# Sync waits between the indirect DMAs of GpSimd, in a kernel of two graph layers

## The chip, the cores and the metric

The kernel runs on one core of one Trainium2 chip. The metric is device time in microseconds (us) of one execution; a kernel is timed in several runs and the median is compared. Engines are named as the profile names them: PE (TensorE matmul), PEld (its weight load), DVE (VectorE), ACT (ScalarE), POOL (GpSimd), SP (SyncE).

## The reference

Sixteen graphs of 1024 nodes with 64 channels go through two residual layers. Each layer begins with a layer norm and a ReLU.

```python
# --- layer 0 ---
h = jnp.maximum(_layernorm(x, axis=-1), 0.0)
x = x + _L0_gnn_ref(h, adj, nodemask, W1, b1, W2, b2)
# --- layer 1 ---
h = jnp.maximum(_layernorm(x, axis=-1), 0.0)
x = x + _L1_gnn_ref(h, adj, ...)
```

Layer 0 thins out the edges of every node with over ten neighbours, and then takes, for each node and each channel, three quantiles (0.25, 0.5, 0.75) over the node's remaining neighbours; their weighted sum is the aggregate:

```python
vals = jnp.where(nd[..., None], x[:, None, :, :], jnp.inf)
s = jnp.sort(vals, axis=2)
for tau, w in zip(TAUS, WTS):
    ...
    agg = agg + w * (v_lo + frac * (v_hi - v_lo))
out = (1.0 + EPS_GIN) * x + agg
y = jax.nn.relu(out @ W1 + b1) @ W2 + b2
```

Layer 1 is three graph convolutions over the full adjacency, relu(adj @ (x @ W) + b) with a batch norm after each, and a last matmul over the three results.

## The kernel before

The graphs are worked in eight pairs. `prepare` loads the adjacency of a pair, thins the edges, counts each node's remaining neighbours and sorts the nodes by that count, so that nodes with few neighbours stand first. `place` holds the sorted place of each node. Nodes are then sorted in groups with a fixed number of slots, one slot for one neighbour's row.

Most groups (`BLOCKS`, `TAIL`) are gathered by one-hot matmuls on PE (`gather`, L1180, from selections made on DVE at L1149). Three groups of nodes (`NODES`, with 17, 19 and 21 slots) are gathered by indirect DMA instead. `fetch_nodes` makes the tile `g_nodes` and a generator `ask`: for each slot k and each of the G parts a of the group (G = 2) it issues one indirect DMA from POOL (L1293) that fetches 128 rows of 64 floats from `rows_d` in DRAM by the indices in `rows_listed`. There are 20 such series over the kernel (`NODE_ORDER`), 744 DMAs in all. `weave` interleaves the steps of these generators with the steps of the sorting networks on DVE (L1087), by shares of the work that are written down in the calls. `sorted_by[0]` is the newest DVE instruction of a sorting network at the time a step is asked for; the first DMA of a slot (a == 0) is made to wait for it, except in the first series, which is asked for before any sorting has begun. `sort_nodes` sorts the rows of `g_nodes`.

The aggregates go to DRAM (`agg_d`) in sorted order. For layer 1, `later` runs beside the last sorting: its function `load` fetches the aggregates of a pair back into node order with one indirect DMA for each of the eight row tiles t of each of the two graphs x, 16 per pair and 128 in all (L1486), within `tc.high_priority()`. `first_layer` adds them to h (L1383), and `next_layer` does the convolutions (L1441).

Other work is issued from POOL too: `live_d` (L894, an indirect scatter of the thinned adjacency into sorted order) and `lp` (L909, its reload).

The instructions are written in the order of the program text, and a scheduler then sets the order on each engine from the dependences and priorities. A dependence can be added by hand with `tc.add_manual_dep`; of the class Sync it becomes a wait on a semaphore. DMAs of POOL use eight completion semaphores in turn.

Of the kernel before, what the change touches and what calls it, by code (L numbers as in the profile page):

```python
# [407 lines left out]
def graph_layers_kernel(ctx: ExitStack, tc: tile.TileContext, ins, out: bass.AP):  # L408
    nc = tc.nc
# [183 lines left out]
    def rows_of(ap):  # L593
        return ap.rearrange("(t p) c -> p t c", p=P)
# [426 lines left out]
    def view(bufs, spec, n1, n2, inner=None):  # L1021
# [20 lines left out]
            dims += [[s2 * W, n2]] * (n1 == 1 and n2 == 1) + [[inner, W // inner], [1, inner]]  # L1042
        return bass.AP(tensor=ap.tensor, offset=ap.offset, ap=dims)

    plans = {}
    sorted_by = [None]

# [232 lines left out]
    def fetch_nodes(pairs, i, pools, tag):  # L1280

        work, ps, rows = pools
        j0, j1, _, slots = NODES[i]
        G = len(pairs) if i == 2 else 2
        pool = work if tag == "s" else keep if tag == "r0" else rows
        g = pool.tile([P, slots, G * C], F32, tag=tag, bufs=2 if tag == "s" else 1, name="g_nodes")

        def ask():
            for k in range(slots):
                for a in range(G):  # L1290
                    st = pairs[a if i == 2 else 0]
                    at = 4 if i == 2 else 2 * a + i
                    asked = nc.gpsimd.indirect_dma_start(  # L1293
                        out=g[:, k, a * C : (a + 1) * C],
                        out_offset=None,
                        in_=rows_d[st.p][:, :],
                        in_offset=bass.IndirectOffsetOnAxis(ap=st.listed[:, at, k : k + 1], axis=0),
                    )
                    if a == 0 and sorted_by[0] is not None:
                        tc.add_manual_dep(  # L1300
                            asked.ins, sorted_by[0].ins.name,
                            mybir.DependencyInfo(mybir.DependencyClass.Sync, mybir.DependencyReason.DATA),
                            reason="rows are asked for one by one",
                        )
                yield

        z = work.tile([P, len(TAUS), G], F32, tag="z_nodes", bufs=2, name="z_nodes")
        for a in range(G):
            st = pairs[a if i == 2 else 0]
            at = 4 if i == 2 else 2 * a + i  # L1310
            nc.scalar.copy(z[:, :, a : a + 1], st.nodes_z[:, :, at : at + 1])
        return pairs, i, g, z, Steps(ask())

    def asking(fetched, first, end, share=1.0):
# [63 lines left out]
    def first_layer(pools, xt, h, agg, mask):  # L1378


        one, ps = pools
        X = xt.shape[2]
        nc.vector.tensor_tensor(agg, agg, h, ALU.add)  # L1383
        oT = channels_first(pools, agg, "chan")
        yield
        for x in range(X):
            rows = slice(x * C, (x + 1) * C)
            hT = one.tile([HID, N], F32, tag="hT", name="hT")
            for hf in range(NH):
                sl = slice(hf * HALF, (hf + 1) * HALF)  # L1390
                pm = ps.tile([HID, HALF], F32, tag="mm", name="pm1")
                nc.tensor.matmul(out=pm, lhsT=w1[rows, :], rhs=oT[rows, sl], start=True, stop=True)
                nc.scalar.activation(hT[:, sl], pm, AF.Relu, bias=b1)
            py = ps.tile([P, NT, C], F32, tag="mm", name="py")
            for t in range(NT):
                nc.tensor.matmul(out=py[:, t, :], lhsT=hT[:, t * P : (t + 1) * P], rhs=w2, start=True, stop=True)
            nc.vector.tensor_tensor(h[:, :, x, :], py, b2[:, None, :].to_broadcast([P, NT, C]), ALU.add)
            yield
        nc.vector.tensor_tensor(h, h, mask[:, :, :, None].to_broadcast([P, NT, X, C]), ALU.mult)
        nc.vector.tensor_tensor(xt, xt, h, ALU.add)  # L1400
        flat = "p t x c -> p (t x) c"
        layernorm_relu(one, agg.rearrange(flat), xt.rearrange(flat), h.rearrange(flat), NT * X)
        yield
        return channels_first(pools, agg, "chan")
# [64 lines left out]
    def later(pools, keep, done):  # L1469

        one, ps = pools


        def load(p):
            assert p < done.sent
            xt = one.tile([P, NT, 2, C], F32, tag="xt", bufs=2, name="xt")
            h = one.tile([P, NT, 2, C], F32, tag="h", name="h_late")
            agg = one.tile([P, NT, 2, C], F32, tag="agg", name="agg")
            mk = one.tile([P, NT, 2], U8, tag="mk", name="mk")
            for x in range(2):  # L1480
                b = 2 * p + x
                nc.sync.dma_start(out=xt[:, :, x, :], in_=rows_of(x_d[b]))
                nc.sync.dma_start(out=h[:, :, x, :], in_=rows_of(h_d[b][:, :]))
                with tc.high_priority():
                    for t in range(NT):
                        nc.gpsimd.indirect_dma_start(  # L1486
                            out=agg[:, t, x, :],
                            out_offset=None,
                            in_=agg_d[b][:, :],
                            in_offset=bass.IndirectOffsetOnAxis(ap=place[:, b, t : t + 1], axis=0),  # L1490
                        )
                nc.sync.dma_start(out=mk[:, :, x], in_=mask_d[b])
            return xt, h, agg, mk

        def first(xt, h, agg, mk):
            mask = one.tile([P, NT, 2], F32, tag="mask", name="mask")
            nc.vector.tensor_copy(mask, mk)
            cur = yield from first_layer(pools, xt, h, agg, mask)
            return xt, cur

        def second(p, x2, cur):
            adjT = []
            for x in range(2):
                adjT.append(one.tile([P, NT, N], F8, tag=f"adjT{x}", name=f"adjT{x}"))
                nc.sync.dma_start(out=adjT[x], in_=adjT_d[2 * p + x][:, :, :])
            yield
            yield from next_layer(pools, [out[2 * p], out[2 * p + 1]], adjT, x2, cur)

        loaded = load(0)
        yield  # L1510
        given = yield from first(*loaded)
        for p in range(NP):
            now = Steps(second(p, *given))
            now.step()
            yield
            ahead = None
            if p + 1 < NP:
                loaded = load(p + 1)
                for _ in range(5):
                    now.step()  # L1520
                    yield
                ahead = Steps(first(*loaded))
            while now.step():
                yield
                if ahead is not None and ahead.step():
                    yield
            if ahead is not None:
                ahead.rest()
                given = ahead.result
# [146 lines left out]
    with ExitStack() as stack:  # L1676
# [56 lines left out]
        with ExitStack() as inner:  # L1733
            one = inner.enter_context(tc.tile_pool(name="late", bufs=1))
# [89 lines left out]
```

## Time and profile before

| | us |
|---|---|
| median of 3 runs | 2872.86 |
| lowest, highest | 2872.21, 2877.92 |
| the profiled execution, time | 2872.55 |
| the profiled execution, span from first to last instruction | 2870.7 |
| DVE busy | 2347.0 (82% of the span) |
| PE busy | 2095.5 (73%) |
| ACT busy | 1584.5 (55%) |
| POOL busy | 1517.0 (53%) |

The busy rows of POOL are almost wholly [...] its DMAs: 1123.2 us for `g_nodes`, 189.4 us for `live_d`, 139.0 us for `agg`. The bytes themselves move on the 16 DMA engines, whose mean load is low (the queue of POOL's DMAs takes 9.0% of the 16 engines' span). A row such as "[0.30 <-issue]" behind an instruction tells how long its engine was idle before it, and what ended that.

### The profile page before, as it was taken

Reading aid. Unit: us, or ns where it says so; the run is one execution under the profiler, and the core shown is the slowest. Engines: PE = TensorE matmul, PEld = TensorE weight load, DVE = VectorE, ACT = ScalarE, POOL = GpSimd, SP = SyncE. Lnnn points to the kernel's source line nnn. Section 1 sums busy time; section 2 is a strip of 40 time slices with the busy share of each in tenths; the row PEclk is TensorE's granted clock in tenths of the full one; section 3 lists DMA queues with packets and bytes.
Section 4 is the critical chain, followed back from the end, with each engine's and each line's share of the span. In section 5 each row is a group of like instructions: output and inputs, shape, how many; then the busy total and the mean of one; then the engine's idle time right before and its main releaser. Section 6 shows DMA issues by size and latency. Waiting matters only on the chain.

```text
span 2870.7 us, 59053 instructions
## 1 busy us (share of the span) xinstructions
PE 2095.5 (73%) x23402; PEld 1450.2 (51%) x23402; DVE 2347.0 (82%) x5475; ACT 1584.5 (55%) x3316; POOL 1517.0 (53%) x1155
## 2 busy tenths in 40 slices
PE   1576986996888688778744985898488396437868
PEld 0344763674565366447522663675366263224545
DVE  3217999999989999999999999999699396637943
ACT  2775776687468568847762687588333133122222
POOL 5115374475838546572834275655855748862220
PEclk9888997998999799889966997999798798768989
DMA  3313222332322242233230322322310341211221
GB/s 98 107 33 103 82 77 58 110 89 65 95 74 73 59 116 86 57 79 99 77 77 12 104 89 74 111 74 64 79 26 14 76 82 52 41 39 45 61 60 46
DMA packets 261055, 205.57 MB, mean 72 GB/s; under 512 B 217121, under 2 KB 217249, under 8 KB 256673
## 3 DMA queue, kind: packets, MB, share of 16 engines
q1 hardware_dynamic: 165120, 131.39, 15.8%
q0 software_dynamic: 39680, 62.23, 9.0%
q10 hardware_dynamic: 55968, 8.09, 1.7%
q8 instruction: 185, 3.03, 0.4%
q14 instruction: 102, 0.83, 0.1%
HBM read 148.82 MB, written 52.75 MB: 70 GB/s over the span
## 4 chain that ended last, share of the span: by engine, by line
DVE 31%; PE 13%; POOL 8%; DMA 8%; ACT 7%; issue 4%; ACTq 0%; POOLq 0%; DVEq 0%; SPq 0%
DVE s L1149 5%; DVE t L1087 4%; POOL g_nodes L1293 4%; PE pg L1441 4%; POOL agg L1486 4%; DVE t_nodes L1087 3%; PE pg L1180 3%; DVE g L1087 2%; DVE g_pairs L1087 2%; DVE t_pairs L1087 2%; DMA a<-in_adj 2%; DVE g_nodes L1087 2%; ACT stays L883 2%; DMA g_nodes<-rows_d,rows_listed 2%; DMA agg<-agg_d,place 2%
## 5 line engine op out<-in xcount | busy, mean ns | idle before, releaser
L1293 POOL DMA_INDIRECT g_nodes<-rows_d,rows_listed x744 | 1123.2, 1510 | 874.4 <-DVE prod L1099 312.5
L1180 PE MATMUL pg<-s,hp 128*64 128x248 bf16 (+6 forms) x12048 | 883.0, 299 | 206.2 <-DVE s L1149 151.1
L1180 PEld LDWEIGHTS <-hp 128*64 128x64 bf16 x12048 | 645.6, 113 | 383.0 <-ACT hp L696 76.4
L1149 DVE TENSOR_SCALAR s<-r 128x3200 bf16<-128x3200 bf16 (+19 forms) x856 | 407.4, 525 | 25.9 <-PE pg L1180 23.7
L1441 PE MATMUL pg<-adjT,xw 128*64 128x512 fp8e4 x2304 | 279.1, 391 | 39.9 <-ACT xw L1430 32.7
L894 POOL DMA_INDIRECT live_d<-edge,place x128 | 189.4, 1480 | 146.9 <-DVE place L886 109.1
L1486 POOL DMA_INDIRECT agg<-agg_d,place x128 | 139.0, 1086 | 190.7 <-DMA agg_d<-agg_nodes 59.1
L1441 PEld LDWEIGHTS <-xw 128*64 128x64 bf16 x2304 | 135.7, 112 | 165.3 <-ACT xw L1430 39.6
L1185 ACT COPY g<-pg 128x248 f32<-128x248 f32 (+3 forms) x238 | 97.0, 408 | 213.1 <-PE pg L1180 212.3
L781 ACT ACTIVATE edge<-a 128x1024 fp8e4<-128x1024 uint32 x128 | 135.5, 1058 | 92.3 <-DMA a<-in_adj 75.5
L788 PE MATMUL ptE<-ident_h,one 128*128 128x128 bf16 x1024 | 84.8, 233 | 114.9 <-DVE one L785 69.2
L1087 DVE TENSOR_TENSOR t<-g 128x800 f32<-128x800 f32 (+9 forms) x184 | 167.5, 923 | 0.8
L1087 DVE TENSOR_TENSOR g<-t 128x992 f32<-128x992 f32 (+7 forms) x176 | 160.2, 931 | 2.0
L864 ACT ACTIVATE edge<-q,bias 128x1024 fp8e4<-128x1024 f32 x128 | 142.2, 1112 | 31.4 <-PE q L859 31.1
L1383 DVE TENSOR_TENSOR agg<-agg,h_late 128x1024 f32<-128x1024 f32 x8 | 9.8, 1229 | 182.2 <-DMA agg<-agg_d,place 182.2
L883 ACT ACTIVATE stays<-keys,minus 128x1024 fp8e4<-128x1024 f32 x128 | 143.1, 1118 | 27.2 <-PE keys L875 26.1
L837 ACT ACTIVATE stays<-cs,back 128x1024 f16<-128x1024 f32 x128 | 137.5, 1113 | 28.3 <-PE cs L833 17.0
L791 ACT ACTIVATE edgeT<-ptE 128x1024 fp8e4<-128x1024 f32 x128 | 131.2, 1028 | 15.5 <-PE ptE L788 14.6
L788 PEld LDWEIGHTS <-one 128*128 128x128 fp8e4 x1024 | 66.0, 104 | 140.2 <-DVE one L785 86.3
L1087 DVE TENSOR_TENSOR t_nodes<-g_nodes 128x256 f32<-128x256 f32 (+6 forms) x192 | 124.2, 658 | 14.4 <-DMA g_nodes<-rows_d,rows_listed 13.8
L929 PE MATMUL pt<-ident_h,lp 128*128 128x128 bf16 x1024 | 88.2, 239 | 58.9 <-ACT liveT L932 30.2
L1445 ACT ACTIVATE xT<-pg,c_L_gnn_b 128x512 f32<-128x512 f32 x48 | 32.9, 686 | 176.6 <-PE pg L1441 176.6
(245 smaller groups left out, 4622.2 us busy)
## 6 DMA issues: line engine op xcount, KB each, us to landing
a<-in_adj SPq DMA_DIRECT2D x128, 512.0 KB
adjT_d<-edgeT SPq DMA_DIRECT2D x16, 1024.0 KB
lp<-live_d POOLq DMA_DIRECT2D x32, 512.0 KB
adjT<-adjT_d SPq DMA_DIRECT2D x16, 1024.0 KB
g_nodes<-rows_d,rows_listed POOLq DMA_INDIRECT x744
room<-in_x SPq DMA_DIRECT2D x16, 256.0 KB
h_d<-room SPq DMA_DIRECT2D x16, 256.0 KB
rows_d<-room SPq DMA_DIRECT2D x64, 64.0 KB
```

Of the source, the lines that this page charges most:

```text
L781: nc.scalar.activation(edge[:, t, :], a[:, :].bitcast(U32), AF.Sign, accum_out=found[:, 0, b, t : t + 1], saturate=False)
L788: nc.tensor.matmul(out=pt[:, u, :], lhsT=one[:, u * P : (u + 1) * P], rhs=ident_h, start=True, stop=True)
L837: nc.scalar.activation(stays[:, t, :], cs, AF.Abs, bias=back[:, t : t + 1], scale=2.0)
L864: nc.scalar.activation(edge[:, t, :], q, AF.Relu, bias=bias(-2.0), accum_out=nv[:, t : t + 1], saturate=False)
L883: nc.scalar.activation(junk, keys, AF.Sign, bias=minus[:, t : t + 1], accum_out=above[:, t : t + 1], saturate=False)
L894: sent = nc.gpsimd.indirect_dma_start(out=live_d[b][:, :], out_offset=bass.IndirectOffsetOnAxis(ap=place[:, b, t : t + 1], axis=0), in_=ed ...
L1087: sorted_by[0] = nc.vector.tensor_tensor(view(bufs, o, n1, n2), view(bufs, a, n1, n2), view(bufs, b, n1, n2), ALU.max if op else ALU.min)
L1149: nc.vector.tensor_scalar(s[:, k, :, us, w0:], r[:, :, us, at + w0 : at + W], float(LIVE + 1 + k0 + k), None, ALU.is_equal)
L1180: summed = nc.tensor.matmul(out=pg[x * C : (x + 1) * C, ks, w0:], lhsT=st.hp[:, part, x, u, :], rhs=s[:, ks, x, u, w0:], start=(whole and ...
L1293: asked = nc.gpsimd.indirect_dma_start(out=g[:, k, a * C : (a + 1) * C], out_offset=None, in_=rows_d[st.p][:, :], in_offset=bass.IndirectO ...
L1441: nc.tensor.matmul(out=pg[cs, :], lhsT=part[:, u, cs], rhs=adjT[x][:, u, sl], start=(u == 0 and k == 0), stop=(u == NT - 1 and k == len(xw ...
L1486: nc.gpsimd.indirect_dma_start(out=agg[:, t, x, :], out_offset=None, in_=agg_d[b][:, :], in_offset=bass.IndirectOffsetOnAxis(ap=place[:, b ...
```

## The change

A helper `wait_for` makes one instruction wait for another with a Sync dependence. The wait for `sorted_by[0]` now goes through it. In `ask`, the first DMA of every odd slot from slot 3 on is also made dependent on `last`, the DMA issued just before it in the program text. In `load`, the DMA of row tile t = 4 of each graph is made dependent on that of row tile t = 3. In the changed file the lines of `ask` stand 8 lower (L1301) and that of `load` 7 lower (L1493).

```diff
+    def wait_for(one, other):
+
+        tc.add_manual_dep(
+            one.ins, other.ins.name,
+            mybir.DependencyInfo(mybir.DependencyClass.Sync, mybir.DependencyReason.DATA),
+            reason="indirect DMAs come with pauses",
+        )
+
...
                     if a == 0 and sorted_by[0] is not None:
-                        tc.add_manual_dep(
-                            asked.ins, sorted_by[0].ins.name,
-                            mybir.DependencyInfo(mybir.DependencyClass.Sync, mybir.DependencyReason.DATA),
-                            reason="rows are asked for one by one",
-                        )
+                        wait_for(asked, sorted_by[0])
+                    if a == 0 and k % 2 and k > 1:
+                        wait_for(asked, last)
+                    last = asked
                 yield
...
                 with tc.high_priority():
                     for t in range(NT):
-                        nc.gpsimd.indirect_dma_start(
+                        asked = nc.gpsimd.indirect_dma_start(
                             out=agg[:, t, x, :],
                             out_offset=None,
                             in_=agg_d[b][:, :],
                             in_offset=bass.IndirectOffsetOnAxis(ap=place[:, b, t : t + 1], axis=0),
                         )
+                        if t == 4:
+                            wait_for(asked, last)
+                        last = asked
                 nc.sync.dma_start(out=mk[:, :, x], in_=mask_d[b])
```

## The prediction, as it was made before the changed kernel had run

> **What bounds the kernel now.** I read four views in this order: the page's chain that ended last (where an added wait could count at all), the costliest groups (what POOL's indirect DMAs cost), the waits (who waits for their landing), and the time line of POOL with the piecewise chain around the DMAs that the change touches.
>
> ```profile
> PE 2095.5 (73%) x23402; PEld 1450.2 (51%) x23402; DVE 2347.0 (82%) x5475; ACT 1584.5 (55%) x3316; POOL 1517.0 (53%) x1155
> DVE 31%; PE 13%; POOL 8%; DMA 8%; ACT 7%; issue 4%; ACTq 0%; POOLq 0%; DVEq 0%; SPq 0%
> L1293 POOL DMA_INDIRECT g_nodes<-rows_d,rows_listed x744 | 1123.2, 1510 | 874.4 <-DVE prod L1099 312.5
> L1486 POOL DMA_INDIRECT agg<-agg_d,place x128 | 139.0, 1086 | 190.7 <-DMA agg_d<-agg_nodes 59.1
> ```
>
> DVE is the busiest engine and holds the largest share of the chain. POOL is busy half the time and holds 8% of the chain: in places it does set the pace. The last two rows (count, busy us, mean ns, idle before) give what one indirect DMA costs POOL, 1510 ns for a row of `g_nodes` and 1086 ns for one of `agg`.
>
> Now the waits (total us, times, longest) of POOL and of DVE:
>
> ```profile
> POOL g_nodes L1293 <- DMA g_nodes<-rows_d,rows_listed: 22.3, 73, 0.3
> POOL agg L1486 <- DMA agg<-agg_d,place: 5.5, 18, 0.3
> DVE agg L1383 <- DMA agg<-agg_d,place: 182.2, 8, 64.1
> ```
>
> POOL's indirect DMAs already wait for earlier ones: with eight completion semaphores in turn, each waits for the one eight issues ahead. The longest such idle is 0.3 us, the ordinary gap between two issues, so that wait never held POOL. The third row is where POOL's pace does count: DVE stands still 182.2 us in all, once for each pair, until the last of that pair's 16 `agg` DMAs has landed.
>
> **The change, step by step.** What counts is how the built program places the waits, so I read the changed kernel's instruction order with its waits against the old one. On PE, ACT, DVE and SP the instructions stand in the same order. On POOL there are 22 more semaphore-wait instructions (590 for 568) and a local reordering. Three things differ from what the diff suggests.
>
> First, only one of the 20 `g_nodes` series is changed, the first, whose DMAs do not wait for `sorted_by`. In the other 19 the built program keeps only the wait for DVE, on the same instructions and values as before; the second dependence leaves no wait. So there are 7 new waits (slots 3, 5, ... 15 of 17) and 16 for `agg` (two for each of 8 pairs), 23 and not 172: series of 17, 19 and 21 slots would hold 7, 8 and 9 waits, and 8 x 7 + 8 x 8 + 4 x 9 + 16 = 172.
>
> Second, in all 23 the scheduler has moved four other indirect DMAs between the one waited for and the one that waits. The waiting one is issued fifth behind it, not next.
>
> Third, the order of the `agg` DMAs within a pair is permuted, but the waits for the aggregates' stores still stand on the first of the 16, and the DVE add needs all 16.
>
> *Price of one wait.* The pace of issue and the time to landing, from the last `agg` group (time line of POOL, then the chain in order of time: start, us, what):
>
> ```profile
> 2769.24 0.94 POOL L1486 DMA_INDIRECT agg<-agg_d,place  x1 [0.30 <-issue]
> 2770.48 0.94 POOL L1486 DMA_INDIRECT agg<-agg_d,place  x1 [0.30 <-issue]
> 2771.73 0.94 POOL L1486 DMA_INDIRECT agg<-agg_d,place  x1 [0.31 <-issue]
> ...
> 2771.73 2.52 DMA agg<-agg_d,place
> ...
> 2039.16 4.96 DMA g_nodes<-rows_d,rows_listed
> ```
>
> One issue every 1.25 us (0.94 busy, 0.30 gap); landing 2.52 us after the issue began. A wait for the DMA just ahead would cost 2.52 - 1.25 = 1.27 us. A wait for the fifth ahead asks for something that was issued 5 x 1.25 = 6.25 us ago and landed 3.7 us ago: it costs nothing. The slowest landing on the chain, 4.96 us while other loads ran, still leaves 1.3 us; and where an issue between them is slower than 0.94 us, the distance grows with it. Cost of 23 waits: 0. What hides them is those four issues; without them it would be 16 x 1.27 = 20 us on DVE's wait for `agg`.
>
> *Price of an extra semaphore instruction.* In the second series the ninth DMA waits for one semaphore and the tenth for two, so that a separate semaphore instruction stands before the tenth:
>
> ```profile
> 342.08 1.66 POOL L1293 DMA_INDIRECT g_nodes<-rows_d,rows_listed  x1 [0.30 <-issue]
> 344.04 1.67 POOL L1293 DMA_INDIRECT g_nodes<-rows_d,rows_listed  x1 [0.30 <-DVE g L1087]
> L1486 POOLq EVENT_SEMAPHORE  x29: 17/43/25597, 2042.3 to 2753.2; - x29
> ```
>
> Both gaps are 0.30 us, so the instruction hides in the gap. The last row (all instructions on `agg`: min/median/max ns) gives the upper end, 43 ns if nothing hid it: 22 x 0.043 = 0.9 us. The lower end is 0; a gain is not excluded, as some old waits fall away, but cannot exceed the same 0.9 us. I take 0.1 us.
>
> *What is queued behind.* First series: its 34 DMAs and their reader on DVE,
>
> ```profile
> 278.66 0.94 POOL L1293 DMA_INDIRECT g_nodes<-rows_d,rows_listed  x1 [0.30 <-issue]
> 328.37 1.82 POOL L1293 DMA_INDIRECT g_nodes<-rows_d,rows_listed  x1 [48.76 <-DVE prod L1099]
> 291.87 0.42 DVE L1087 TENSOR_TENSOR t_nodes<-g_nodes 128x256 f32<-128x256 f32 x1
> ```
>
> The last lands at about 278.66 + 2.5 = 281.2, DVE first reads at 291.87 without an idle time before it, and POOL then stands idle 48.76 us. Some 10 us of slack: even 7 waits of 1.27 us (8.9 us) would fit. Nothing gets late here. `agg`: the two waiting DMAs of a pair have only other `agg` DMAs of that pair behind them, and in some pairs `g_nodes` rows; who waits is the DVE add at L1383. Nothing is added, so nothing there is later.
>
> Sum: 0 + 0 + 0.1 us against the profiled execution's 2872.55 (span 2870.7 and 1.85 around it), which lies 0.3 us below the median of 2872.86. Forecast: 2873.0.
>
> **A rule that speaks against "no change".** The chain holds some very long issues:
>
> ```profile
> 2027.27 10.15 POOL g_nodes L1293
> 2055.76 5.69 POOL agg L1486
> ```
>
> Both fall while DVE sorts; in the last `agg` group, where DVE stands idle, all issues take 0.94 to 0.96 us. The Trainium skill, in "SBUF — State Buffer", section "Who interferes with whom", says that VectorE and GpSimd share a pair of SBUF ports, that a VectorE instruction in a two-port mode takes the pair for its whole length and blocks the other, and that the order of issue decides who is blocked. The rows fit a blocking of this kind but do not show which instruction did it. By the rule, moving POOL's issues by even tens of ns can redeal who is blocked: one such issue on the chain more or fewer is 5.69 - 0.94 = 4.8 us, the time 2877.8 or 2868.2. By the rows alone it is 0. I keep 0, since the changed places are few and the last group has no DVE work beside it, and keep 4.8 us for the range.
>
> **The rivals.**
>
> (a) *It works as the diff reads*: 172 waits of 1.27 us, each on the DMA just ahead. On `agg` all are on DVE's wait: 20 us. Of the `g_nodes` issues the chain holds 4% of the span, 115 of 1123 us, a tenth; 156 x 1.27 x 0.1 = 20 us. Time 2913. For it: only the program text. Against it: the built order. 2%.
>
> (b) *The fifth-ahead wait bites* (ends slower). Place: the `agg` groups that run beside heavy loads. It decides once a landing takes more than 5 x 1.25 = 6.25 us: to lose 5.7 us over 16 waits each must last 0.36 us, a landing of 6.6 us. The slowest seen on the chain is 4.96 us, and the wait eight ahead never bit. If landings were 7.5 us: 16 x 1.25 = 20 us, 2893. 3%.
>
> (c) *Blocked issues are redealt*: one or two long issues more, 2878 to 2883 (4% beyond the bound), or fewer, 2863 to 2868 (4%).
>
> (d) *The pauses help*: fewer DMAs in flight, shorter issues. The excess of the `agg` issues is 139.0 - 128 x 0.94 = 18.7 us; a third of it gone would be 2867. But no pause of any length is made. 1%.
>
> **How the numbers follow.** The runs before spread from 2872.21 to 2877.92, and 0.2% is 5.7 us: about what a measurement of this kernel can tell from no change. No change: 86%, predicted 2873.0. Slower by over 0.2%: (a) 2, (b) 3, (c) 4, 9%. Faster by over 0.2%: (c) 4, (d) 1, 5%. The range, 2868 to 2879, holds the forecast with the spread of runs and one redealt issue either way.
>
> **What would show it right or wrong.** Right: in the changed profile the `agg` and `g_nodes` issues keep gaps of 0.30 us, the POOL rows that wait for `g_nodes` or `agg` DMAs keep a longest of 0.3 us, DVE's wait for `agg` stays near 182 us in 8, and the first series still ends about 280 us. Wrong: single POOL idles of 0.5 us or more released by an `agg` DMA (b); 1.2 us gaps in later `g_nodes` series (a); or these all the same and another count of issues over 4 us on the chain (c).

## The result, and the profile after

| | before | after |
|---|---|---|
| median, us | 2877.44 (12 runs) | 2877.36 (12 runs) |
| lowest, highest | 2871.19, 2885.97 | 2866.57, 2882.93 |
| profiled execution, us (span) | 2872.55 (2870.7) | 2877.09 (2875.3) |

The ratio is 0.9994, with a 95% interval of 0.9979 to 1.0009: no change that can be measured. The forecast was 2873.0 us. The 4.5 us between the two profiled executions is no effect: the 12 runs of either kernel spread over 15 to 16 us. A ratio, here and below, is estimated from the runs within 1.5% of the fastest of the same kernel, so it can differ from the quotient of the medians (below, on the chip of e0, only 26 of 70 runs of the kernel before lie within).

The page after, in the rows shown of before (busy time and share of each engine; the chain that ended last, by engine; the two groups of POOL's indirect DMAs with count, busy us, mean ns and the idle before them):

```profile
PE 2088.5 (73%) x23402; PEld 1446.9 (50%) x23402; DVE 2346.6 (82%) x5475; ACT 1584.1 (55%) x3316; POOL 1524.3 (53%) x1155
DVE 32%; PE 14%; ACT 8%; DMA 8%; POOL 6%; issue 4%; ACTq 0%; POOLq 0%; DVEq 0%; SPq 0%
L1301 POOL DMA_INDIRECT g_nodes<-rows_d,rows_listed x744 | 1136.8, 1528 | 874.6 <-DVE prod L1107 313.4
L1493 POOL DMA_INDIRECT agg<-agg_d,place x128 | 138.7, 1083 | 187.5 <-DVE g_nodes L1095 59.2
```

An `agg` issue takes 1083 ns for 1086, a `g_nodes` issue 1528 for 1510, and the idle time before the `g_nodes` group is 874.6 for 874.4 us. The waits after (us in all, times, longest):

```profile
DVE agg L1390 <- DMA agg<-agg_d,place: 186.2, 8, 67.8
POOL g_nodes L1301 <- DMA g_nodes<-rows_d,rows_listed: 26.5, 87, 0.3
POOL agg L1493 <- DMA agg<-agg_d,place: 7.6, 25, 0.3
```

POOL waits for an `agg` DMA 25 times where it was 18, and for a `g_nodes` DMA 87 times where it was 73. The counts also differ between two executions of the kernel before (21 and 82 in `b0_before`, below), so they do not show the new waits by themselves. What counts is the longest, 0.3 us, which is the gap between two issues in any case: the new waits hold nothing up.

The semaphore instructions of POOL on the two lines (min/median/max ns, first and last start; the `g_nodes` line of before first):

```profile
L1293 POOLq EVENT_SEMAPHORE  x354: 17/17/8772, 184.0 to 2563.4; - x177
...
L1301 POOLq EVENT_SEMAPHORE  x360: 17/17/8768, 185.6 to 2573.6; - x180
L1493 POOLq EVENT_SEMAPHORE  x45: 17/43/25695, 2039.8 to 2767.9; - x45
```

Before, they were 354 and 29: 6 and 16 more, the 22 that the built program has. The count agrees with one changed series, but does not prove it: a wait need not take an instruction of its own, and `e8_nodes_next` (below) has 146 new `g_nodes` waits with 363 such instructions. The waits were counted in the built program: 7 on `g_nodes` and 16 on `agg`, all on the DMA five issues ahead. Last, the end of the first series and its first reader, and the last `agg` group (time line: start, us, what, idle before), and that group's landing on the chain:

```profile
277.30 0.94 POOL L1301 DMA_INDIRECT g_nodes<-rows_d,rows_listed  x1 [0.31 <-issue]
326.56 1.82 POOL L1301 DMA_INDIRECT g_nodes<-rows_d,rows_listed  x1 [48.33 <-DVE prod L1107]
...
289.99 0.42 DVE L1095 TENSOR_TENSOR t_nodes<-g_nodes 128x256 f32<-128x256 f32 x1
...
2766.66 0.94 POOL L1493 DMA_INDIRECT agg<-agg_d,place  x1 [0.30 <-issue]
2767.91 0.95 POOL L1493 DMA_INDIRECT agg<-agg_d,place  x1 [0.31 <-DMA agg<-agg_d,place]
2769.16 0.94 POOL L1493 DMA_INDIRECT agg<-agg_d,place  x1 [0.30 <-issue]
...
2775.40 2.47 DMA agg<-agg_d,place
```

The first series still ends about 280 us. The `agg` DMA at 2767.91 is released by an earlier `agg` DMA and starts 0.31 us behind its neighbour, like those released by nothing.

### The profile page after: what moved, and what is told of

It reads as the page before. It is cut to its first block, busy times and chain, and to the rows that moved or that the text cites. A ratio compares the mean times of both kernels' runs of the same rounds, so it can differ in the third digit from the quotient of the medians.

```text
span 2875.3 us, 59074 instructions
## 1 busy us (share of the span) xinstructions
PE 2088.5 (73%) x23402; PEld 1446.9 (50%) x23402; DVE 2346.6 (82%) x5475; ACT 1584.1 (55%) x3316; POOL 1524.3 (53%) x1155
## 4 chain that ended last, share of the span: by engine, by line
DVE 32%; PE 14%; ACT 8%; DMA 8%; POOL 6%; issue 4%; ACTq 0%; POOLq 0%; DVEq 0%; SPq 0%
DVE s L1157 5%; DVE t L1095 5%; PE pg L1448 4%; POOL agg L1493 3%; PE pg L1188 3%; DVE t_nodes L1095 3%; DVE g L1095 3%; POOL g_nodes L1301 3%; DVE t_pairs L1095 3%; DVE g_pairs L1095 2%; DMA a<-in_adj 2%; ACT liveT L932 2%; ACT stays L883 2%; DMA agg<-agg_d,place 2%; DVE g_nodes L1095 2%
## 5 line engine op out<-in xcount | busy, mean ns | idle before, releaser
L1301 POOL DMA_INDIRECT g_nodes<-rows_d,rows_listed x744 | 1136.8, 1528 | 874.6 <-DVE prod L1107 313.4
L894 POOL DMA_INDIRECT live_d<-edge,place x128 | 183.6, 1434 | 148.4 <-DVE place L886 110.6
L1493 POOL DMA_INDIRECT agg<-agg_d,place x128 | 138.7, 1083 | 187.5 <-DVE g_nodes L1095 59.2
```

What stands on the lines that cost most here:

```text
L894: sent = nc.gpsimd.indirect_dma_start(out=live_d[b][:, :], out_offset=bass.IndirectOffsetOnAxis(ap=place[:, b, t : t + 1], axis=0), in_=ed ...
L1301: asked = nc.gpsimd.indirect_dma_start(out=g[:, k, a * C : (a + 1) * C], out_offset=None, in_=rows_d[st.p][:, :], in_offset=bass.IndirectO ...
L1493: asked = nc.gpsimd.indirect_dma_start(out=agg[:, t, x, :], out_offset=None, in_=agg_d[b][:, :], in_offset=bass.IndirectOffsetOnAxis(ap=pl ...
```

## The experiments

All edits are made to the kernel before. `wait_for` is the helper of the change; `behind` fixes an order on the engine without a semaphore:

```python
def behind(one, other):
    tc.add_manual_dep(
        one.ins, other.ins.name,
        mybir.DependencyInfo(mybir.DependencyClass.NoSync, mybir.DependencyReason.SCHED_ONLY),
        reason="in the order of the text",
    )
```

On the chip that ran the first four (e0, e1, e3, e4) every kernel, that of before too, took about 3.1 ms in place of 2.88 ms; those four were run again on other chips (as e9, e12, e8, e10), and what follows rests on the later runs. A ratio is always to the kernel before on the same chip.

### The order alone, and waits five issues ahead

The built change differs from its text in two ways: a distance of five issues, and a moved order. `e9_order` (first `e0_order`) only holds each indirect DMA behind the one before it in the text, for `g_nodes` and `agg`; `e10_fifth` (first `e4_fifth`) adds 391 waits in the same order, each on the DMA five issues ahead, 17 times as many as the 23 of the change.

```diff
+                    if asks:
+                        behind(asked, asks[-1])
+                    if a == 1 and len(asks) > 4:       # e4, e10 only
+                        wait_for(asked, asks[-5])
+                    asks.append(asked)
...
+                        if asks:
+                            behind(asked, asks[-1])
+                        if len(asks) > 4:              # e4, e10 only
+                            wait_for(asked, asks[-5])
+                        asks.append(asked)
```

Expected of e0:

> No new wait at all: each indirect DMA of a g_nodes series and of a pair's 16 agg DMAs is only made to stand behind its predecessor in POOL's order (no semaphore). 376 places of POOL's order change, no other engine's order does. My theory (only a wait that POOL really stands in costs anything): no change, 0.998 to 1.002. Rival (the order in which POOL's issues meet DVE's work redeals which of them are blocked): a shift of several long issues, 5 to 15 us either way (0.995 or 1.005).

Expected of e4:

> The waits of the change, many times over: every agg DMA and every second g_nodes DMA waits for the fifth ahead, in the order of the text: 391 waits at distance five instead of 23, no other engine's order changes. Theory (the fifth ahead has landed): longest POOL idle for such a DMA stays 0.3 us, ratio 0.998 to 1.002. Rival (b) of the prediction (it bites beside heavy loads): idles above 0.3 us; at 0.36 us each on 89 agg waits 32 us, ratio 1.011. Rival (a satisfied wait costs 43 ns that nothing hides): 17 us of POOL, of which 5 us on the time, 1.002.

Measured: before 3117.81 us on that chip; e0 3134.55, ratio 1.011 (1.0077 to 1.0143; the quotient of the medians is 1.0054); e4 3124.84, 1.0031 (1.0001 to 1.006). With a kernel before that itself took 240 us more than elsewhere, e0 was not the 1.000 expected, and e4 with its waits came out below e0 without. So they were run again.

Expected of e9:

> e0_order once more: the text order on POOL in all 20 g_nodes series and in agg (376 places), no new wait. It is the control for e8_nodes_next, which has the g_nodes part of this order and 153 waits and took 3120 us beside 2877 us of the kernel before. Theory (the waits are the cause): within 0.3% of the kernel before, DVE's wait for g_nodes under 20 us. Rival (the order is the cause, since e0_order and e3_nodes_next took about the same time in the first set, 3135 and 3126 us): the same 1.085 here.

Expected of e10:

> e4_fifth once more: the same order with 391 waits, each on the DMA issued five ahead. Theory (what was waited for has landed by then): equal to e9_order within 0.3%, POOL's waits for g_nodes and agg DMAs no longer than 0.3 us but for a few. Rival (the wait bites where landings are slow): up to 0.5 us x 391 = 196 us more, 1.068 of e9_order.

Measured: before 2879.19; e9 2891.91, 1.0043 (1.0027 to 1.0059); e10 2896.70, 1.0068 (1.0051 to 1.0084). The order by itself costs 12.7 us, more than the 0.3% expected. The 391 waits add 4.8 us to that; the intervals of the two overlap, so this is not told from nothing, and it would be 4.8 / 391 = 12 ns for a wait. The waits of `t_nodes` in `b0_before` and in e9, then those of e10, of `t_nodes` and of POOL:

```profile
DVE t_nodes L1087 <- DMA g_nodes<-rows_d,rows_listed: 8.8, 2, 4.6
DVE t_nodes L1103 <- DMA g_nodes<-rows_d,rows_listed: 32.0, 2, 17.1
...
DVE t_nodes L1103 <- DMA g_nodes<-rows_d,rows_listed: 32.7, 2, 17.1
POOL g_nodes L1310 <- DMA g_nodes<-rows_d,rows_listed: 16.2, 53, 0.3
POOL agg L1509 <- DMA agg<-agg_d,place: 6.5, 13, 2.8
```

In e10 a single wait for a `g_nodes` or `agg` DMA is longer than the gap (2.8 us). DVE's longer wait for `g_nodes` comes with the order: it is there in e9 already, 32.0 us against 8.8 in the kernel before on another chip (`b0_before`, below) and 13.8 in its first profiled execution. That is 18 to 23 us more, but DVE's wait for `agg` is 24 us shorter in e9 (160.2 for 184.1). So where the 12.7 us arise is not shown, and which moved DMA does it was not tried.

The 391 waits take few instructions of their own, as in the built program most replace the old wait on the DMA eight ahead: on the lines of `g_nodes` and `agg` stand 365 and 46 semaphore instructions in e10 and 325 and 31 in e9, 55 more in all.

### The same waits on the issue just ahead, in the later series

`e3_nodes_next`, and the same file again as `e8_nodes_next`: the text order in `g_nodes`, and the second DMA of each odd slot from slot 3 on waits for the one just ahead, in all 20 series. There are 153 waits on the issue just ahead, of which 146 are new (the first DMA of seven series has one in the kernel before too).

```diff
+                    if asks:
+                        behind(asked, asks[-1])
+                    if a == 1 and k % 2 and k > 1:
+                        wait_for(asked, asks[-1])
+                    asks.append(asked)
```

Expected of e3:

> The wait in all 20 g_nodes series, at distance one: put on the second DMA of every odd slot from slot 3 on, which has no other added dependence, waiting for the first DMA of the same slot, and the series are held in the order of the text; agg as before. 153 waits at distance one in the built program (7 of them old ones), no other engine's order changes. Theory: each is a POOL idle of 1.2 to 1.3 us, 185 us in all; a tenth of POOL's g_nodes time lies on the chain, so 19 us, ratio 1.004 to 1.010. Rival 1 (POOL has room, it idles 874 us ahead of g_nodes): the waits are there but the time stays, 0.998 to 1.002. Rival 2 (pauses shorten the issues): POOL's busy time on g_nodes falls below 1100 us and the time with it, 0.995.

Measured on the first chip: 3126.45, 1.0058 (1.0035 to 1.0082), and less than e0, the order without waits, there. Expected of the repeat:

> e3_nodes_next once more on this chip: 153 g_nodes DMAs wait for the one just ahead. POOL should again stand idle about 150 times for 2.2 us, 330 us in all. Theory (a tenth of the g_nodes issues lie on the chain): 33 us slower than the kernel before, 1.011, if the order by itself costs nothing. Rival (the sorting on DVE sets the pace of these series, so that POOL's pauses are only taken from its idle time before the next slot): within 0.2%, and POOL's idle time behind DVE shrinks by what the pauses take.

Measured: before 2877.21; e8 3120.01, 1.0855 (1.0821 to 1.089), 243 us slower. Both theories were far off. The order costs 12.7 us (e9), so the waits cost about 230 us. The time line of POOL in one of the series, and the waits; then the page's row of `g_nodes` (busy us, mean ns, idle before) in e9 and in e8:

```profile
974.21 0.94 POOL L1310 DMA_INDIRECT g_nodes<-rows_d,rows_listed  x1 [0.30 <-issue]
976.76 1.06 POOL L1310 DMA_INDIRECT g_nodes<-rows_d,rows_listed  x1 [1.60 <-DMA g_nodes<-rows_d,rows_listed]
978.12 0.96 POOL L1310 DMA_INDIRECT g_nodes<-rows_d,rows_listed  x1 [0.30 <-issue]
979.38 1.25 POOL L1310 DMA_INDIRECT g_nodes<-rows_d,rows_listed  x1 [0.30 <-issue]
980.93 1.51 POOL L1310 DMA_INDIRECT g_nodes<-rows_d,rows_listed  x1 [0.30 <-issue]
984.11 1.19 POOL L1310 DMA_INDIRECT g_nodes<-rows_d,rows_listed  x1 [1.68 <-DMA g_nodes<-rows_d,rows_listed]
...
POOL g_nodes L1310 <- DMA g_nodes<-rows_d,rows_listed: 319.3, 148, 6.3
DVE t_nodes L1103 <- DMA g_nodes<-rows_d,rows_listed: 219.6, 20, 35.8
...
L1310 POOL DMA_INDIRECT g_nodes<-rows_d,rows_listed x744 | 1134.5, 1525 | 916.9 <-DVE g L1103 293.1
L1310 POOL DMA_INDIRECT g_nodes<-rows_d,rows_listed x744 | 1121.1, 1507 | 1160.1 <-DMA g_nodes<-rows_d,rows_listed 319.3
```

One issue in four starts 1.6 us or more after the end of its neighbour. The mean is 319.3 / 148 = 2.16 us, of which 0.30 is the ordinary gap: 1.86 us for a wait, 148 x 1.86 = 275 us. POOL's idle time before `g_nodes` grows by 243 us (916.9 to 1160.1), so only some 30 us of the pauses come out of idle time that POOL had in any case. DVE's sort then waits 219.6 us for its rows, in 20 places, where it was 32.0 in two in e9: more than four fifths of the pauses (230 of 275) arrive at the end. Where it was lost: the first `agg` add of layer 1 starts at 2270.9 us in e8 and at 2087.8 in e9, 183 of the 230 us, before layer 1 has begun; the other part falls among the eight pairs.

Why the same pauses (330.9 us in 149) cost nothing beside e0 on the first chip is not settled. The program of e3 and e8 took about the same on both chips (3126 and 3120 us); it is e0 that took 3135 us there, where the same program took 2892 in e9. TensorE stood idle in e0 with nothing seen to end it; the row in e0, in e9 and in e8:

```profile
PEld L1196 <- issue: 238.8, 362, 17.2
...
PEld L1196 <- issue: 73.8, 131, 17.2
...
PEld L1196 <- issue: 66.9, 91, 17.2
```

The kernel before has 68.1 us in that row in `b0_before`; e3 has 90.3 on the first chip. So the 243 us of e8 are not this idle. An idle of another kind that had already slowed e0 could take up the pauses of e3, but no run varied it.

### The waits that the change really makes, without the distance

`e11_first_next` makes the seven waits of the first series, each on the issue just ahead. No instruction moves on any engine.

```diff
+                    if asks and sorted_by[0] is None:
+                        behind(asked, asks[-1])
+                    if a == 0 and k % 2 and k > 1 and sorted_by[0] is None:
+                        wait_for(asked, asks[-1])
+                    asks.append(asked)
```

> The seven waits that the change really makes on g_nodes (first series, slots 3 to 15), but each on the DMA issued just ahead, with no instruction moved on any engine. Theory (10 us of slack before DVE's first read hides them): POOL stands idle 7 times for 1.6 to 2.2 us, the series ends 9 to 13 us later than before, DVE reads at about 292 us as before or at most 3 us later, and the time is that of the kernel before within 0.2%. Rival (in the later series nearly the whole of such waits reached the end, 228 us for 153 in e8_nodes_next beside e9_order, 1.5 us each): 7 x 1.5 = 10 us, 1.0036.

Measured: before 2875.72; e11 2877.33, 1.0017 (0.9996 to 1.0038). By the time alone the rival's 1.0036 is not excluded. The time line decides (POOL's second, sixth and last of the seven pauses, the last issue of the series and the first of the next, and the first two reads on DVE):

```profile
246.43 1.19 POOL L1310 DMA_INDIRECT g_nodes<-rows_d,rows_listed  x1 [2.62 <-DMA g_nodes<-rows_d,rows_listed]
...
279.07 1.16 POOL L1310 DMA_INDIRECT g_nodes<-rows_d,rows_listed  x1 [3.20 <-DMA g_nodes<-rows_d,rows_listed]
...
287.36 1.01 POOL L1310 DMA_INDIRECT g_nodes<-rows_d,rows_listed  x1 [2.91 <-DMA g_nodes<-rows_d,rows_listed]
...
292.09 1.65 POOL L1310 DMA_INDIRECT g_nodes<-rows_d,rows_listed  x1 [0.30 <-issue]
327.36 1.82 POOL L1310 DMA_INDIRECT g_nodes<-rows_d,rows_listed  x1 [33.61 <-DVE prod L1115]
...
290.55 0.42 DVE L1103 TENSOR_TENSOR t_nodes<-g_nodes 128x256 f32<-128x256 f32 x1
...
296.05 0.42 DVE L1103 TENSOR_TENSOR t_nodes<-g_nodes 128x256 f32<-128x256 f32 x1
```

The seven idles are 2.25, 2.62, 1.74, 1.72, 1.75, 3.20 and 2.91 us, together 16.2; less seven gaps of 0.30 the series is 14.1 us later, and it ends at 293.7 where it was 279.6. DVE begins at 290.55 all the same, without an idle before it, while the last issues are still to come: its first read cannot need them. The next series begins at 327.36, no later than the 328.37 of before, and POOL's idle ahead of it has shrunk from 48.76 to 33.61 us: the pauses came out of that. A wait of about 2 us, seven times, is hidden here, where the same wait costs about 1.6 us in the later series (230 us for 146).

### The same for agg

`e12_agg_next` (first `e1_agg_next`) is the `agg` half of the diff with the text order, so that ten of the 16 waits are on the issue just ahead. `e2_agg_each` lets each `agg` DMA but the first wait for the one ahead (75 more waits on the issue just ahead than before, 25 on the one two ahead). `e7_agg_text` is the text order on POOL without the waits.

```diff
+                        if asks:
+                            behind(asked, asks[-1])    # e2: wait_for(asked, asks[-1])
+                        if t == 4:                     # e1, e12 only
+                            wait_for(asked, asks[-1])
+                        asks.append(asked)
```

Expected of e1:

> Only the agg part of the change (t = 4 waits for t = 3), and the 16 DMAs of a pair are held in the order of the text, so that the wait falls on the DMA just ahead: in the built program 10 of the 16 new waits stand at distance one, the others at two to five. My theory (the four issues in between hide the wait): with them gone each of the 10 waits shows as a POOL idle of 1.2 to 1.3 us, and DVE waits longer for agg: 12 us on the time, ratio 1.003 to 1.006. Rival (a wait on POOL is absorbed even at distance one, because the loads of layer 1 have slack): 1.000. The scheduler moves some PE and DVE instructions as well (650 and 239 places), which adds a few us of uncertainty.

Measured on the first chip: 3102.77, 0.9951 (0.992 to 0.9982), against the expectation and not to be read alone. Expected of the others:

> The agg DMAs of a pair are issued in the order of the text (a dependence without a semaphore); no wait is added, and only 64 places of POOL's order differ. Theory (order alone costs nothing): ratio 1.000, within 0.998 to 1.002; DVE's wait for agg stays 180 to 190 us in 8. Rival (moved issues are redealt against VectorE's work, as e0_order's 1.011 could mean): 1.004 to 1.011, with more agg issues over 4 us.

> In the text order each agg DMA but the first of a pair waits for the one ahead of it: 77 waits on the issue just ahead, 25 on the one two ahead, 18 on others. Theory (a wait on the issue just ahead stops POOL until that one has landed, and for agg that is on DVE's wait): 77 x 1.27 us, the price of the prediction, gives 98 us; 77 x 2.2 us, the mean idle that e3_nodes_next showed, 169 us. DVE's wait for agg grows from 182 us to 280 to 350 us and the time by as much, 1.034 to 1.06 of before. Rival (the wait is taken up by later work, since DVE's wait is once a pair and the scheduler moves other work of PE, DVE and ACT around it): DVE's wait grows, but the time by less than 0.5%.

> e1_agg_next once more: in the text order the fifth agg DMA of each graph waits for the fourth; 10 of the 16 waits are on the issue just ahead. Theory (an agg wait lengthens DVE's wait for agg and so the time): 10 x 1.27 = 13 us by the price of the prediction, 10 x 1.5 = 15 us by the 116 us that 77 such waits cost in e2_agg_each; 1.0045 to 1.005. Rival (the moved work of PE and DVE around the pairs decides, 650 and 239 places, or the wait is taken up): 0.998 to 1.001.

Measured: e7 2878.01 beside 2877.21, 1.0005 (0.9993 to 1.0017): this order costs nothing that can be measured. e2 2993.63, 1.0402 (1.038 to 1.0424), 116 us slower, which would be 116 / 75 = 1.55 us for a wait on the issue just ahead, were all of it theirs. e12 2885.81 beside 2875.72, 1.0033 (1.0016 to 1.0051), 10 us slower, or one for each of its ten such waits. DVE's wait in `b0_before`, the waits of e2, then of e12; last, PE's wait for the DVE add in the first profile of the kernel before and in e2:

```profile
DVE agg L1383 <- DMA agg<-agg_d,place: 184.1, 8, 66.5
...
POOL agg L1503 <- DMA agg<-agg_d,place: 153.0, 96, 4.0
DVE agg L1399 <- DMA agg<-agg_d,place: 244.7, 8, 59.2
...
POOL agg L1503 <- DMA agg<-agg_d,place: 25.1, 24, 3.4
DVE agg L1399 <- DMA agg<-agg_d,place: 209.2, 8, 74.8
...
PE pt L1372 <- DVE agg L1383: 63.2, 1, 63.2
PE pt L1388 <- DVE agg L1399: 247.4, 6, 67.1
```

POOL's waits hold it now, up to 3.4 and 4.0 us where 0.3 was the longest. DVE's wait for `agg` grows from 184.1 us (`b0_before`) to 244.7 and 209.2. In e2 only 61 of the 116 us show in that row; in e12 the row grows by 25 us and the time by 10. The scheduler also moved work of PE and DVE in e12 and e2, which e7 leaves in place, and in e2 PE waits for the DVE add 247.4 us where it was 63.2. So the waits of `agg` do hold POOL, but how much of the 10 and the 116 us is theirs, and how much comes from the moved work, is not separated.

### The kernel before, once more

> The kernel before, once more, as its own control and for a profile from the same chip as the three kernels beside it. Every theory expects a ratio of 1.000, and its interval is what this chip can tell. In the first set of four experiments all kernels, that of before too, took about 3118 us and TensorE's weight loads of the row gather alone stood idle 239 us with nothing seen to end the idle (70 us in the profile before). If that lies with the chip, this profile shows either the 70 us and a time near 2877, or the 239 us and a time near 3118, with no change of the program.

Measured: 2873.87 beside 2877.21, 0.9991 (0.9977 to 1.0005). What this run tells is in the issues of `agg` (min/median/max ns):

```profile
L1486 POOL DMA_INDIRECT agg<-agg_d,place x128: 940/944/3241, 2059.8 to 2772.1; - x128
```

The same program had a longest of 5686 ns in its first profiled execution and has 3241 here; the changed kernel has 6378. So the length of the longest issue does not tell the two programs apart.

## Why the prediction was right

*One series of 20, 23 waits, at distance five.* This was read from the built program. The trace agrees: 6 and 16 more semaphore instructions, and no wait of over 0.3 us in any series, so none on the issue just ahead (in e8 these show as 1.6 us and more). A satisfied wait in a later series would not show. Why the second dependence leaves no wait in the 19 others was not settled.

*A wait on the fifth ahead costs nothing.* Shown, with POOL's longest wait at 0.3 us in the changed kernel, and with 17 times as many waits by e10 beside e9. What rival (b) feared shows in one `agg` wait of e10 (2.8 us).

*The extra semaphore instruction.* Taken at 0.1 us for all 22, with 43 ns each as the upper end. No run measures it: e10 has 55 more of them than e9 and is 4.8 us slower, which is not told from nothing. Were it all theirs, it would be 87 ns each and 1.9 us for the 22.

*The slack of the first series.* The conclusion held, the term was too small: 7 x 1.27 = 8.9 us was put against 10 us of slack; without the distance the pauses are 14.1 us (e11). They fit because the first read does not need the last rows. For these seven waits the distance was not needed at all; what it hides lies at most in the 16 of `agg`.

*What the four issues hide.* For `agg` 16 x 1.27 = 20 us was named as the cost without them. e12 is 10 us slower with ten such waits (and six at two to five issues), about the size named, but with other engines' work moved too.

*Blocked issues redealt.* The Trainium skill's rule of the shared port ("SBUF — State Buffer", "Who interferes with whom") was weighed as up to 4.8 us for a moved place. Blocking by a single DVE instruction does not account for the 5.69 us issue: the longest on DVE in that time are two of 0.86 us (start, us of both, what):

```profile
2057.46 1.72 DVE L1149 TENSOR_SCALAR s<-r 128x3072 bf16<-128x3072 bf16 x2
```

One long issue stands in the first `agg` group on the chain after, too, in which only a part counts (start, us, what):

```profile
2056.24 4.32 POOL agg L1493
```

But the longest `agg` issue differs as much between two executions of one program (5.69 and 3.24 us) as between the two kernels. No run shows that the change redealt any; its moved places cost nothing that can be measured, and those of e7 neither. What makes an issue long stays open.

*Rival (a), that the diff does what it says*, was rightly given little chance but was badly mis-sized. The forecast was 20 us for 156 `g_nodes` waits and 2913 us with `agg`; e8, with 146 new waits on the issue just ahead, shows about 230 us. Two terms of that sum failed. 1.27 us came from a quiet `agg` group at the end, while the `g_nodes` pauses, beside other work, are 1.86 us each. And the tenth was the share of `g_nodes` issues on the chain, where more than four fifths of the pauses arrived.

*The level.* That the forecast of 2873.0 us lies 4.4 us below the measured time is not the change's doing: it was built on three runs with a median of 2872.86, and twelve runs of the same kernel have 2877.44. The twelve spread over 15 us, about 0.5%, more than the 0.2% that was taken for what a measurement can tell. That 2877.36 still lies 1.6 us inside the range is in part luck.

## What to carry to other kernels

A wait written in the program text costs what its place in the built order makes of it: count the issues between the two DMAs and set them against the time to landing, before anything else. The share of an engine on the chain tells what it costs now, not what a delay of it would cost: work that ends just before its reader is largely exposed once it is later (in e8, 32.0 us of DVE's wait became 219.6), while work with a long idle behind it is not (the first series in e11). Take the price of a wait from the stage where it stands, not from a quiet one.

## What the runs showed that was not expected

One chip took 3117.81 us for the kernel before, where the four other measurements gave 2875.72 to 2879.19. On it the same program (e0 beside e9) had 238.8 us for 73.8 in TensorE's idle without a releaser at the row gather, and the same two programs (order, order with pauses) that differ by about 230 us elsewhere took nearly the same time. The granted clock was 0.85 there and 0.88 on the others, but e8, at 3120 us on one of the others, had 0.85 too. The cause stays open. And the order of POOL's DMAs alone, with no wait added, cost 12.7 us.
